# Eight of the sixteen states of a selective scan moved into the linear attention before it

## The chip, the cores and the metric

The kernel runs on one core of a Trainium2 chip. The metric is the device time of one execution in microseconds (us). The engines are named as the profile names them: PE (TensorE matmuls; PEld its weight loads), DVE (VectorE), ACT (ScalarE), POOL (GpSimd) and SP (SyncE, which here only issues DMAs). Each engine works through its own instructions in order, and semaphores tie them together.

## What is computed

Eight blocks follow one another on x of shape (4, 1024, 128), each as `x = layernorm(x + block(x))`: a gated recurrence, a routed slot memory, a sampled attention, a gated feed-forward, and then the four that matter here. All of it is float32.

```python
# L2 attention: causal linear attention, 16 heads of 64, over T positions
S += k_t[:, None] * v_t[None, :];  out_t = (q_t @ S) / max(q_t @ z, 1e-6)   # cos and sin weighted
# L2 feed-forward: each row goes to 2 of 8 experts (a gated MLP), weighted sum of the two
# L3 attention: a selective scan, E = 256 channels, N = 16 states each
delta = softplus(xs @ wd1.T @ wd2.T + wd2_b);  A = -exp(A_log)
Bm = xs @ wb.T;  Cm = xs @ wc.T
def step(h, inp):
    h = exp(d_l[:, :, None] * A) * h + (d_l * x_l)[:, :, None] * b_l[:, None, :]
    y_l = einsum('ben,bn->be', h, c_l)
y = (y + xs * W_D) * silu(skip);  out = resid + y @ out_w.T
# L3 feed-forward: 8 experts with hidden size 512, kept up to a probability mass of 0.8
```

The sum over the 16 states in `y_l` has no order of its own: each state is a recurrence for itself.

## The kernel before, in words

**The linear attention** (`l2_attn`) works through 128 units: four batch elements, four quarters of 256 positions each, eight pairs of heads. A loop over t writes the PE instructions of several units in a fixed order: keys of unit t+1 (`l2_keys`), projections of t+2 (`l2_project`, tile `pqk`), scores of t+1 (`l2_scores`, tile `pa`, which DVE weights into `a` at L1122), sums of t (`l2_before`, `l2_within`, tile `po`) and of t+1 (`l2_sums`, tile `st`). In `l2_project` ACT makes `r_q` and `r_k` (L1056) and POOL multiplies `r_q` into `qt` (L1064), which `l2_before` reads two rounds later. PE's order in this part is written out by hand; every other engine's order, and all of what comes later, is made by a scheduler when the program is built, by priority and by its own idea of times.

**The pairs of the L2 feed-forward** are prepared while the attention runs. When an element's attention is finished, `l2_dispatch` routes its rows (a chain of small DVE steps) and puts each row twice into a buffer in HBM, sorted by expert: 16 indirect DMAs on POOL's queue (`xrows`, L1388), one a round. `l2_ffn` is one generator over the 92 tiles of all elements (23 each): SP loads a tile's weights (`wx`, L1463), PE, ACT and DVE compute it (`pa_m` or `ph` from `xgT`, `kp_mo` or `py` from `mh`), `yrows` goes to HBM, and `l2_combine` gathers an element's rows back: per half of an element eight indirect DMAs on POOL's queue (`yg`, L1534), scaling on ACT, an addition and a norm. Inside the attention `early` moves this generator one step a round. It waits whenever the next element has not been put, and then holds back the last eight tiles of the element before it. `m2["rest"]` is the last element's put loop.

**The scan** (`l3`) goes through eight halves (element, then 512 positions). For each, `l3_prepare` makes the norm, the convolution, the step sizes `dl`, the inputs `ud` and the rows of B and C, which go to HBM (`rows`). `l3_scan` then does 16 states, each so: SP loads one row of B and one of C to all partitions (`bn`, `cn`, L1849); POOL multiplies `db = ud * bn` (L1854, 128x1024); for each of two channel halves ACT makes the decay `da = exp(dl * aneg)` in PSUM (L1858) and DVE runs the recurrence (L1859) from `da` and `db` into `db`; POOL multiplies `hc = db * cn` (L1870). PE adds the `hc` of all states into PSUM by a matmul with the identity (`pys`); from element 1 on two states are first added by an accumulating DMA (`hc<-hc`, L1875). `l3_sum` and `l3_finish` end the half, and then its experts can start (`l3_experts`, `ph`, `hh`, `py` from `wh`, at most four steps beside one state). The first half of all is prepared inside the attention, one step a round (`l3_early`, `l3_prepare`), from the round on in which element 0's pairs are all combined (`st["done"]`); its 16 states follow after the attention. `l3_early` keeps that half's tiles in the feature copies `xT` of the elements whose attention is over.

## Time and profile before

| | us |
|---|---|
| median of 6 executions | 2316.08 (2309.01 to 2318.73) |
| the profiled execution | 2313.36 |
| its span, first to last instruction | 2311.6 |
| PE busy | 2007.9 (87%) |
| DVE busy | 1352.4 (59%) |
| ACT busy | 1192.5 (52%) |
| POOL busy | 1023.8 (44%) |

In the profiled execution the linear attention's units begin at about 614 us; their last norm ends at about 1344; the first `db` of half 0 begins at 1388.7, of half 1 at 1486.0, of half 2 at 1576.0, and the last `hc` ends at 2172.3. Times in the text are counted from the first instruction. A share of busy time is a mean over stages that have different limits, so the windows of single stages say more than the table.

### The profile page before, as it was taken

What the parts mean: (1) busy time and instruction counts of PE and PEld (TensorE: products, weight loads), DVE (VectorE), ACT (ScalarE), POOL (GpSimd) and SP (SyncE); (2) the same over time, 40 slices, a digit from 0 to 9 for tenths busy, and PEclk for the clock granted to TensorE, in tenths of its full rate; (3) what the DMA queues carried; (4) which work ended last, traced back from release to release, by engine and by line L of the source; (5) the groups of instructions that cost most, each with busy time, mean ns of one, the idle gap of its engine ahead of it and who ended that gap; (6) DMA issues with size and microseconds to landing.
All of it is one profiled execution on the core that took longest, in us unless ns stands there. A gap on an engine that the chain in (4) does not pass through costs nothing.

```text
span 2311.6 us, 46313 instructions
## 1 busy us (share of the span) xinstructions
PE 2007.9 (87%) x17788; PEld 1403.9 (61%) x17788; DVE 1352.4 (59%) x3668; ACT 1192.5 (52%) x2606; POOL 1023.8 (44%) x812
## 2 busy tenths in 40 slices
PE   6679789989999999999979866688888899898998
PEld 3555465544477777787768654346565556565666
DVE  6658544343455654654645555785776788777521
ACT  6533334322244444454555546476767886767443
POOL 5100310000123244234143337987788889888500
PEclk9668879989999999999989987799999999999999
DMA  3000110050000010021222065455676667676411
GB/s 106 0 28 10 40 38 1 19 172 0 1 3 2 3 38 22 25 88 43 76 77 79 22 202 166 123 176 168 197 219 173 173 186 199 179 196 175 118 60 51
DMA packets 138555, 211.09 MB, mean 91 GB/s; under 512 B 18596, under 2 KB 75933, under 8 KB 137950
## 3 DMA queue, kind: packets, MB, share of 16 engines
q1 hardware_dynamic: 126190, 173.87, 24.4%
q0 software_dynamic: 12144, 34.26, 7.1%
q8 instruction: 140, 2.29, 0.4%
q14 instruction: 81, 0.66, 0.1%
HBM read 160.29 MB, written 23.16 MB: 79 GB/s over the span
## 4 chain that ended last, share of the span: by engine, by line
PE 44%; DVE 13%; ACT 11%; issue 3%; another core or an unknown queue 1%; POOL 1%; DMA 1%; SPq 0%; ACTq 0%; DVEq 0%; POOLq 0%
PE py L129 8%; PE ph L129 7%; PE po L1131 5%; PE pa_m L129 5%; DVE db L1859 5%; PE pqk L129 5%; PE kp_mo L129 3%; PE pys L129 3%; PE pv L129 2%; PE pr L1201 2%; ACT hh L1985 1%; PE pt L133 1%; ACT da L1858 1%; PE kp_mo L133 1%
## 5 line engine op out<-in xcount | busy, mean ns | idle before, releaser
L1064 POOL TENSOR_TENSOR qt<-r_q,sb_c_turn 128x256 f32<-128x256 f32 (+1 forms) x256 | 164.4, 662 | 455.0 <-ACT r_q L1056 450.8
L1870 POOL TENSOR_TENSOR hc<-db,cn 128x1024 f32<-128x1024 f32 x128 | 317.6, 2516 | 84.1 <-PE pys L129 41.5
L129 PEld LDWEIGHTS py<-wh,hh 128*128 128x128 f32 x2048 | 253.5, 194 | 83.8 <-issue 45.9
L1854 POOL TENSOR_TENSOR db<-ud,bn 128x1024 f32<-128x1024 f32 x112 | 289.8, 2657 | 12.4 <-issue 9.9
L129 PE MATMUL ph<-xT,wh 128*128 128x512 f32 x512 | 255.5, 614 | 26.2 <-DVE h_acc L2001 8.4
L129 PE MATMUL py<-wh,hh 128*128 128x128 f32 x2048 | 261.2, 279 | 16.3 <-ACT hh L1985 8.0
L1985 ACT ACTIVATE hh<-ph,sb_cols 128x512 f32<-128x512 f32 x256 | 170.5, 681 | 131.9 <-PE ph L129 100.0
L1122 DVE TENSOR_TENSOR a<-pa_m,sb_c_near 128x256 f32<-128x256 f32 x256 | 96.6, 419 | 210.4 <-PE pa_m L129 198.2
L1079 ACT ACTIVATE kN<-kp_mo,sb_c_trig 128x128 f32<-128x128 f32 x448 | 129.8, 371 | 131.3 <-PE kp_mo L133 122.9
L1858 ACT ACTIVATE da<-dl,aneg 128x512 f32<-128x512 f32 x224 | 153.4, 689 | 78.3 <-DVE db L1859 74.7
L129 PE MATMUL pys<-hc,sb_c_ident 128*128 128x512 f32 x324 | 157.9, 617 | 16.8 <-POOL hc L1870 14.6
L1859 DVE TENSOR_TENSOR_SCAN db<-da,carry,db 128x512 f32<-128x512 f32 x128 | 157.1, 1265 | 13.1 <-ACT da L1858 9.4
L1859 DVE TENSOR_TENSOR_SCAN db<-da,db 128x512 f32<-128x512 f32 x128 | 149.4, 1204 | 9.3 <-POOL db L1854 5.2
L129 PEld LDWEIGHTS ph<-xT,wh 128*128 128x128 f32 x512 | 88.5, 194 | 107.7 <-issue 54.0
L2001 DVE SCALAR_TENSOR_TENSOR h_acc<-py,gt,h_acc 128x128 f32<-128x128 f32 x256 | 71.9, 342 | 131.3 <-PE py L129 129.3
L129 PE MATMUL pqk<-xT,wE 128*128 128x256 f32 x512 | 135.7, 388 | 8.3 <-ACT coT L1198 4.2
L129 PEld LDWEIGHTS pys<-hc,sb_c_ident 128*128 128x128 f32 x324 | 60.8, 200 | 79.3 <-issue 58.0
L129 PEld LDWEIGHTS pqk<-xT,wE 128*128 128x128 f32 x512 | 88.2, 192 | 21.8 <-DVE cv L1041 6.6
L1198 ACT COPY coT<-pt 128x512 f32<-128x512 f32 x64 | 37.5, 586 | 115.9 <-PE pt L133 115.9
L129 PE MATMUL po<-ht,wD 128*128 128x512 f32 x192 | 93.3, 598 | 0.0
L1131 PE MATMUL po<-cv,a 128*64 128x65 f32 x2048 | 89.2, 230 | 0.0
L844 DVE TENSOR_SCALAR ht<-ph,sb_cols 128x512 f32<-128x512 f32 x48 | 35.7, 749 | 90.3 <-PE ph L129 90.2
(453 smaller groups left out, 4311.3 us busy)
## 6 DMA issues: line engine op xcount, KB each, us to landing
wx<-in_wF SPq DMA_DIRECT2D x92, 384.0 KB
bn<-rows SPq DMA_DIRECT2D x128, 256.0 KB
cn<-rows SPq DMA_DIRECT2D x128, 256.0 KB
wh<-in_wH SPq DMA_DIRECT2D x64, 512.0 KB
hc<-hc POOLq DMA_DIRECT2D x47, 512.0 KB
xrows<-zero SPq DMA_DIRECT2D x4, 1472.0 KB
xg<-xrows SPq DMA_DIRECT2D x20, 256.0 KB
yrows<-ys SPq DMA_DIRECT2D x20, 256.0 KB
```

Of the source, the lines that this page charges most:

```text
L129: return self.nc.tensor.matmul(out=out, lhsT=lhsT, rhs=rhs, start=start, stop=stop)
L133: self.nc.tensor.transpose(out, in_, self.ident[0:n, 0:n])
L1064: nc.gpsimd.tensor_mul(u["qt"][:, m, a:], u["q"][:, a:], c2["turn"][:, m, o + a : o + 2 * P])
L1079: self.nc.scalar.activation(u["kN"][:, c, m, :], pk[:, c, :], AF.Copy, scale=trig[:, k, m : m + 1])
L1122: nc.vector.tensor_mul(u["a"][:, i, :, :], pa[i], self.c2["near"][:, None, :].to_broadcast([P, 2, P]),)
L1131: self.nc.tensor.matmul(out=u["po"][self.HALF[j], i, c, :], lhsT=lhsT, rhs=rhs, start=key not in u["begun"], stop=True, skip_group_check=True,
L1854: nc.gpsimd.tensor_mul(db, ud, bc[0])
L1858: nc.scalar.activation(da, dl[:, ec, :], AF.Exp, scale=aneg[:, j : j + 1])
L1859: nc.vector.tensor_tensor_scan(db[:, ec, :], da, db[:, ec, :], carry[:, ec, n : n + 1] if h else 0.0, ALU.mult, ALU.add,)
L1870: nc.gpsimd.tensor_mul(hc, db, bc[1])
L1985: nc.scalar.activation(ht, ph, AF.Relu, bias=self.col("h_b1", i=e * NK + k))
L2001: nc.vector.scalar_tensor_tensor(acc[:, c, :], py[:, c, :], gt[:, c, e : e + 1], acc[:, c, :], ALU.mult, ALU.add,)
```

## The change

A constant `NEARLY = 8` says how many states of half 0 are taken early. The new generator `l3_first` runs them inside the attention, after `l3_prepare`, about one step a round. Per state it has the two row loads, `db = ud * bn` on POOL, two exponentials on ACT into an SBUF tile `da`, two recurrences on DVE with both inputs in SBUF, the copy of the carry on ACT, and the multiplication by `cn` on POOL. The sum over the states is kept in SBUF (`acc`, in element 0's `xT`): state 0 is multiplied straight into it, and states 1 to 7 are added by accumulating DMAs on POOL's queue, each of which waits for the one before. `bn`, `cn`, `db` and `da` have two buffers each, in a new pool `scan` that lives as long as the attention. `l3_scan` begins at state 8 for that half, and `l3_sum` adds `acc` with two DVE additions.

To have half 0 ready earlier, element 0's pairs run to their end alone (`l2_tiles_of(0, 1)`) before those of elements 1 to 3 begin, its 16 rows are put two a round, and preparing starts when the first half of the element is combined (`st["half"]`). In `l3` half 0 has eight states; beside each of them two steps of half 1's preparation and of the last put loop are taken. `next(moe)` is called twice a state in halves 0 and 1, and once later; before, twice in half 0 and once later. The weights `wA` move out of the constants into the first stage's pool, and the pools `wd` and `w0` are opened earlier. The cut diff:

```diff
+NEARLY = 8
 # l2_attn
-            side, begin = [], None
+            side, begin, left = [], None, 4 * NEARLY
...
-                    if "done" in self.m2["st"][0]:
+                    if "half" in self.m2["st"][0]:
                         if begin is None:
-                            begin = self.l3_prepare(self.l3_early(first))
-                        next(begin, None)
+                            scan = ctx.enter_context(tc.tile_pool(name="scan", bufs=2))
+                            u = self.l3_early(first, scan)
+                            begin = chain(self.l3_prepare(u), self.l3_first(u, scan))
+                        for k in range(1 if "dl" not in u else max(1, -(-left // max(1, n - t)))):
+                            next(begin, None)
+                            left -= 1
 # l2_dispatch
-                yield
+                if k or b:
+                    yield
 # l2_ffn
+        yield from self.l2_tiles_of(0, 1, wp)
+        yield from self.l2_tiles_of(1, B, wp)
+    def l2_tiles_of(self, b0, b1, wp):
-            for st in self.m2["st"]
+            for st in self.m2["st"][b0:b1]
 # l2_combine, after each half
+            st["half"] = h
 # l3
-            for n in range(NST):
+            for n in range(u.get("start", 0), NST):
                 with self.tc.high_priority(offset=1000):
                     next(scan)
                     next(end, None)
-                    next(nxt, None)
-                for k in range(1):
+                    for k in range(1 if i else 2):
+                        next(nxt, None)
+                for k in range(1 if i else 2):
                     next(self.m2["rest"], None)
-                next(moe, None)
-                if i == 0:
-                    for k in range(1):
-                        next(moe, None)
+                for k in range(2 if i < 2 else 1):
+                    next(moe, None)
 # new
+    def l3_first(self, u, pool):
+        nc, aneg = self.nc, self.c3["aneg"]
+        dl, ud, rows, acc, carry = (u[k] for k in ("dl", "ud", "rows", "acc", "carry"))
+        for n in range(NEARLY):
+            bc = []
+            for i, nm in enumerate(("bn", "cn")):
+                t = pool.tile([P, 1, 512], F32, name=nm)
+                r = i * NST + n
+                nc.sync.dma_start(
+                    out=t[:, 0, :], in_=rows[r : r + 1, :].to_broadcast([P, 512])
+                )
+                bc.append(t.to_broadcast([P, 2, 512]))
+            yield
+            db = pool.tile([P, 2, 512], F32, name="db")
+            nc.gpsimd.tensor_mul(db, ud, bc[0])
+            yield
+            for ec in range(2):
+                j = ec * NST + n
+                da = pool.tile([P, 512], F32, name="da")
+                nc.scalar.activation(da, dl[:, ec, :], AF.Exp, scale=aneg[:, j : j + 1])
+                nc.vector.tensor_tensor_scan(
+                    db[:, ec, :], da, db[:, ec, :], 0.0, ALU.mult, ALU.add
+                )
+            nc.scalar.copy(carry[:, :, n : n + 1], db[:, :, 511:512])
+            yield
+            nc.gpsimd.tensor_mul(db if n else acc, db, bc[1])
+            if n:
+                nc.gpsimd.dma_start(out=acc, in_=db, accum_op=ALU.add)
+            yield
 # l3_scan
-        for n in range(NST):
+        for n in range(u.get("start", 0), NST):
 # l3_sum
+            if "acc" in u:
+                self.nc.vector.tensor_add(p, u["acc"][:, ec, :], p)
```

More of the change, by code (lines that the diff above doesn't have):

```diff
@@ L61, with __init__ @@
 class Net:
-    def __init__(self, ctx, tc, io):
+    def __init__(self, ctx, tc, io, wd, w0):
         self.tc, self.nc, self.io = tc, tc.nc, io
@@ L70, in __init__ @@
         c = self.const
+        self.wdp = wd.enter_context(tc.tile_pool(name="wd", bufs=1))
+        self.w0p = w0.enter_context(tc.tile_pool(name="w0", bufs=1))
         self.xN = [c.tile([P, NC, D], F32, name=f"xN{b}") for b in range(B)]
@@ L81, in __init__ @@
             if b == 0:
-                self.wgru = self.load("wA", [P, 4, P])
+                self.wgru = self.load("wA", [P, 4, P], self.w0p)
                 self.cols = self.load("cols", [P, NCOLS])
@@ L1697, in l3_at, with l3_early @@
         return pool.tile(shape, F32, name=name, tag=tag)
-    def l3_early(self, pool):
-        half = lambda b, i: self.xT[b][:, i * 512 : (i + 1) * 512]
+    def l3_early(self, pool, scan):
+        half = lambda i: self.xT[0][:, i * 512 : (i + 1) * 512]
+        two = lambda x: x.rearrange("p (e t) -> p e t", e=2)
         k = [0]
         def at(name, shape):
-            if name in ("xnT", "tail", "xs3"):
+            if name in ("xnT", "tail", "xs3", "ud"):
                 return pool.tile(shape, F32, name=name)
-            if name in ("dl", "ud"):
-                return self.xT[1 if name == "dl" else 2].rearrange("p (e t) -> p e t", e=2)
+            if name == "dl":
+                return two(self.xT[1])
@@ L1710, in at @@
             if name == "sq3":
-                return half(2, 0).rearrange("p (k d) -> p k d", d=D)
+                return half(0).rearrange("p (k d) -> p k d", d=D)
             if name == "db1":
-                return half(2, 1)[0:ND]
+                return scan.tile([P, 512], F32, name="da")[0:ND]
             if name == "xc":
                 k[0] += 1
-                return half(0, k[0] % 2)
-            return half(0, name == "sp_w")[:, None, :]
-        u = dict(b=0, h=0, at=at, ff=self.bank("pj"))
+                return half(k[0] % 2)
@@ L1720, in l3_early @@
+            return half(name == "sp_w")[:, None, :]
+        u = dict(b=0, h=0, at=at, ff=self.bank("pj"), start=NEARLY, acc=two(self.xT[0]))
+        u["carry"] = pool.tile([P, 2, NST], F32, name="carry0")
         self.c3["first"] = u
         return u
+    def l3_first(self, u, pool):
[27 more added lines that the diff above has]
+            yield
@@ L1830, in l3_scan @@
         xnT, xs, dl, ud, rows = (u[k] for k in ("xnT", "xs", "dl", "ud", "rows"))
-        carry = wp.tile([P, 2, NST], F32, name="carry") if h == 0 else u["prev"]["carry"]
-        u["carry"] = carry
+        if "carry" not in u:
+            u["carry"] = (
+                u["prev"]["carry"] if h else wp.tile([P, 2, NST], F32, name="carry")
+            )
+        carry = u["carry"]
         u["py"] = py = []
@@ L2167, in program @@
     with ExitStack() as ctx:
-        n = Net(ctx, tc, io)
         wd, w0 = ExitStack(), ExitStack()
-        wdp = wd.enter_context(tc.tile_pool(name="wd", bufs=1))
-        W = n.l0_load(w0.enter_context(tc.tile_pool(name="w0", bufs=1)))
-        d = n.l1_ffn_load(wdp)
+        n = Net(ctx, tc, io, wd, w0)
+        W = n.l0_load(n.w0p)
+        d = n.l1_ffn_load(n.wdp)
         dp = ctx.enter_context(
```

## The prediction

> **What bounds the kernel now.** I read the page's 40 slices first, then the windows by stage. Columns: PE, PEld, DVE, ACT and POOL busy with instruction counts, granted clock, DMA share, GB/s.
>
> ```profile
> 614.00:1159.00 545.00, 515.30 (x9378) 419.87 (x9377) 308.86 (x1081) 250.00 (x737) 175.22 (x280) 1.00 0.11 33
> 1159.00:1210.00 51.00, 36.10 (x440) 29.62 (x439) 23.81 (x103) 29.47 (x87) 21.00 (x26) 0.83 0.25 73
> 1340.00:1486.00 146.00, 89.28 (x348) 59.51 (x347) 82.90 (x181) 77.43 (x175) 105.27 (x64) 0.74 0.54 166
> 1486.00:1806.00 320.00, 273.40 (x1305) 180.94 (x1303) 233.76 (x442) 219.00 (x423) 266.07 (x144) 0.93 0.62 180
> 1806.00:2172.00 366.00, 338.10 (x1670) 218.82 (x1671) 280.75 (x535) 263.16 (x455) 325.60 (x162) 1.00 0.69 186
> 2172.00:2312.00 140.00, 126.11 (x692) 89.31 (x690) 33.11 (x119) 56.57 (x91) 0.35 (x1) 0.96 0.18 55
> ```
>
> Until 1340 the linear attention runs, and PE sets its pace (515 of 545 us) while POOL is a third busy. From 1486 POOL and PE are both near 90% over the scans of halves 1 to 7. Between lies a hole, 1340 to 1486: PE 89 of 146 us at clock 0.74. There half 0 is scanned, and no expert of the last layer can start before it is finished. Next I read POOL's timeline in the hole (start, length, line, what ended the idle time before).
>
> ```profile
> 1369.97 0.99 POOL L1388 DMA_INDIRECT xrows<-xN,di  x1 [0.30 <-DVE wt L1382]
> 1388.69 2.35 POOL L1854 TENSOR_TENSOR db<-xT,bn 128x1024 f32<-128x1024 f32 x1
> 1399.45 0.99 POOL L1534 DMA_INDIRECT yg<-yrows,di  x1 [0.16 <-issue]
> 1409.20 6.98 POOL L1870 TENSOR_TENSOR hc<-db,cn 128x1024 f32<-128x1024 f32 x3
> 1437.11 6.96 POOL L1870 TENSOR_TENSOR hc<-db,cn 128x1024 f32<-128x1024 f32 x3 [7.59 <-DVE db L1859]
> 1486.00 9.27 POOL L1854 TENSOR_TENSOR db<-ud,bn 128x1024 f32<-128x1024 f32 x4
> ```
>
> The last element's routing ends at 1370, 30 us after the attention; 16 puts (`xrows`) hold POOL until 1390; 16 states, eight gathers and some waits take it to 1486, where half 1 begins. So the hole is POOL's, and the change halves its states. The price must be looked for before 1340.
>
> **What eight states leave out of the hole.** In the changed program's order of instructions POOL has, after the attention: 16 puts, `db` x4, `hc` x3, 8 gathers, `hc`, `db` x4, `hc` x3, 8 gathers, `hc`, then half 1. Counted from the attention's end: routing 30 as now; puts 1370.0 to 1390, 20 us, so 50; the first scan began 12.6 us after the first `db` (1388.7 to 1401.3 in DVE's rows), so 63; three states' scans took 12 us there (1401.3 to 1413.4), plus one `hc` of 2.4, so 77. Eight gathers took 10.1 (1359.9 to 1370.0): 87. One `hc` and four `db`, 11.7: 99. Three `hc`, 7.0, with 2 us for DVE (the waits there were 7.6, 1.8 and 0): 108. Gathers 10.1, `hc` 2.4: half 1 starts after 121 us, not 146, a gain of **25**. With no wait for scans it is 110 (gain 36), with the 7.6 us wait twice 131 (gain 15). The eight gathers more than now between `db` and half 1 belong to element 1, whose pairs now end later; the gain is no 8/16 of the hole for that reason. SP's loads do not push this back: `bn` and `cn` of the first four states stand behind pair tile 45's weights where they now stand behind tile 53's, and they are issued at the routing's end (1369.9) in any case.
>
> **What eight states cost in the attention.** First the attention's units, eight without pair tiles, eight with one each, then the five while element 0's pairs were combined and five like them without that.
>
> ```profile
> 811.40:850.20 38.80, 37.19 (x745) 29.92 (x745) 21.20 (x74) 16.96 (x52) 15.49 (x22) 1.00 0.16 50
> 971.50:1021.40 49.90, 49.34 (x849) 41.99 (x849) 29.34 (x105) 24.54 (x79) 15.46 (x22) 1.00 0.30 91
> 1155.00:1210.30 55.30, 40.40 (x521) 33.40 (x520) 27.86 (x126) 32.12 (x93) 22.42 (x28) 0.85 0.27 80
> 1014.50:1049.50 35.00, 32.64 (x540) 27.18 (x538) 20.10 (x69) 18.84 (x54) 13.59 (x19) 1.00 0.31 89
> ```
>
> A unit is 4.85 us, a tile adds 1.39. The new order runs 34 tiles before the last projection instead of 38: **-5.6**; the four come back in the hole, where PE has 57 us idle. The combination costs 20.3 us now, since 16 gathers stand before `qt` on POOL and ACT waits for them. It moves to units without tiles, where ACT has less else to do; I take **-4** (0 to -10). Preparing half 0 (the norm, convolution and step sizes) moves 20 units forward with the same instructions, tile-free as now: 0. Two puts a unit for element 0: 16 x 1 us spread over eight units of an idle POOL, 0.
>
> The eight states stand in units 106 to 117 of POOL's order. POOL gets 16 multiplies of 2.35 (37.6), 7 accumulating DMAs of 1.08 (row below, 7.6), beside 24 `qt` of 0.73 (17.5) and 8 puts of 0.99 (7.9): 70.6 us in units that now take 12 x 4.85 plus two tiles and a norm, about 62. DVE gets 16 scans. Today's scans read their decay from PSUM (L1859: 1.19 to 1.28 us whatever POOL does); the new ones read decay and input both from SBUF. The nearest rows with that are the first layer's:
>
> ```profile
> 13.99 1.23 DVE L237 TENSOR_TENSOR_SCAN gru_h<-gru_a,gru_z 128x512 f32<-128x512 f32 x1 [3.19 <-POOL gru_z L235]
> 40.53 1.21 DVE L237 TENSOR_TENSOR_SCAN gru_h<-gru_a,gru_z 128x512 f32<-128x512 f32 x1
> 40.78 2.03 POOL L235 TENSOR_TENSOR gru_z<-gru_z,gru_g 128x512 f32<-128x512 f32 x1 [1.90 <-ACT gru_z L231]
> 42.77 1.26 POOL L235 TENSOR_TENSOR gru_z<-gru_z,gru_g 128x512 f32<-128x512 f32 x1
> 42.84 2.27 DVE L237 TENSOR_TENSOR_SCAN gru_h<-gru_a,gru_z 128x512 f32<-128x512 f32 x1 [0.47 <-POOL gru_z L235]
> ```
>
> Alone each takes 1.2 to 1.3 us; together the later one takes 2.0 to 2.3. So the two engines' work adds: 70.6 + 16 x 1.22 = 90 us, less the 15.5 us of DMA issues that read no tile: 75 to 90, I take 80, so **+18** over 62. Behind a held scan on DVE stand `a` and `st`, which PE needs within a unit; behind a multiply on POOL stands `qt`, needed about a unit later, a slack of some 5 us that 18 us exceed. The new waits on POOL: a state's sum waits in POOL's queue until the sum before it has landed, and with two `db` buffers the multiply two states later does too, with `qt` and the puts of element 2 queued behind. Today's `hc` sums have their last packet 4.4 to 6 us after the issue, and states follow at 7 to 10 us, so I count 0 (up to 2 us x 7). On ACT 16 exponentials of 0.69 and 8 copies of 0.18, 12.5 us in units that keep it busy for 17 of 39: 0, or part of the 18 where they delay `r_q`. On SP the 16 `bn` and `cn` loads stand ahead of tile 28's weights, used some six units after the last of them can go: 0. Bounds of the whole: 0 if the slack and the gaps hide all, and 66 if nothing is hidden (8 x (2 x 2.35 + 1.08 + 2 x 1.22) = 8 x 8.2). I stay near the low end, since POOL is idle for two thirds of the attention.
>
> The Trainium skill ("SBUF — State Buffer", "Who interferes with whom") speaks against this edit: a DVE instruction with two SBUF inputs and a GpSimd instruction that reads SBUF exclude each other for a whole instruction. The rows alone would also allow that both run at half speed; a scan beside a 2.35 us multiply would then take 2.4 us, by the page up to 3.6. As an estimate by that page, up to 16 x 1.2 = 19 us more would stand on DVE, and the sum would end near no gain.
>
> **After the hole.** POOL's work from half 1 on is the same 112 states. The tiles are not spread alike: 15 and 14 in halves 1 and 2 become 30 and 0, and element 3's gathers move from half 3 to half 2. Halves 1 to 3 took 100, 108 and 112 us. PE's 81 us in half 1 become 81 + 15 x 1.74 (1.13 + 0.61 a tile in the timeline) = 107, so about 120 us; half 2 loses 24 us of PE and gains 10 of POOL, 106; half 3 loses 20 of POOL, 92 like half 4. 318 against 320: **0** (-10 to +18). POOL's wait there is PE already:
>
> ```profile
> L1870 POOL TENSOR_TENSOR hc<-db,cn 128x1024 f32<-128x1024 f32 x113 | 282.8, 2538 | 72.5 <-PE pys L129 41.5 <-DVE db L1859 11.9 <-DMA bn<-rows 8.0
> L1875 POOL DMA_DIRECT2D hc<-hc x47 | 50.7, 1080 | 0.3 <-POOL hc L1870 0.3
> ```
>
> Sixteen fewer additions on PE lie in the hole, 0; two DVE additions of 0.7 for the sum, 0 beside half 1's scans (1.4 if not). **Sum: -5.6 - 4 + 18 - 25 + 0 = -16.6.** The profiled execution took 2313.36 us (span 2311.6 and 1.8 around it), 2.7 under the median of 2316.08; the shift applied to the median gives **2299**. About 0.2% (4.6 us) is what a measurement can tell.
>
> **Rivals.** *Free cover*: the attention hides the states (+3) and scans keep ahead (-30): -37, 2279. For it: POOL's idle time; against it: the L237 rows. 0.20. *Lockstep*, the slower side: in units 106 to 117 POOL, DVE and PE wait on each other in turn, because `qt` and `a` stand in order behind each state's multiply, scan and landing of the sum before it, and the whole 8.2 us of a state is exposed: 66 - 9.6 - 25 = +31, 2347. It decides from 34.6 us exposed, 4.3 us a state. For it: the combination's 20 us came from just such queueing; against it: idle shares. 0.21. *Half 1 bound by PE*: 30 tiles hold it and half 2 gives nothing back: +18, 2317, no change. 0.11. My forecast has 0.48, its own range 2284 to 2313.
>
> Faster: 0.46 + 0.20 + 0.01 = 0.67; same: 0.02 + 0.08 + 0.01 = 0.11; slower: 0.20 + 0.02 = 0.22. The range reaches into lockstep and free cover: 2274 to 2328.
>
> **What would show it.** Right: attention longer by some 8 us in all, units 106 to 117 near 80 us; scans in SBUF at 1.2 to 3.6 us; hole near 121 us; no pair tile after half 1. Wrong: units 106 to 117 over 97 us, or half 1 over 135 us with half 2 still over 105.

## The result, and the profile after

The changed kernel takes 2324.14 us (22 executions) against 2316.99 (46) before: a ratio of 1.0031 (95% interval 1.0021 to 1.0042), slower, where 2299 was forecast. Its profiled execution took 2323.88 us against 2313.36. The stages below are cut at the same rows of both traces: first projection of the attention (`pqk`), end of its last output projection (`pr`), first `db` of half 1 and of half 4, end of the last multiplication `hc`, last computing instruction.

| stage, us | before | after | difference | forecast |
|---|---|---|---|---|
| up to the first projection | 614.5 | 619.2 | +4.7 | 0 |
| attention | 724.3 | 753.1 | +28.8 | +8.4 |
| from its end to half 1 (the hole) | 147.2 | 108.1 | -39.1 | -25 |
| halves 1 to 3 | 320.6 | 319.8 | -0.8 | 0 |
| halves 4 to 7 | 365.7 | 382.1 | +16.4 | no term |
| after the last `hc` | 135.8 | 136.4 | +0.6 | no term |

The first line is within chance: runs e1 to e4 below, which share the changed kernel's code up to there and ran on one chip, began the attention between 614.7 and 621.1 us. The windows of the changed kernel (columns as before), with the first element's combination, the units with the early states, the hole, and halves 1 to 4:

```profile
1081.00:1128.00 47.00, 32.56 (x414) 23.17 (x407) 14.75 (x53) 18.36 (x55) 27.78 (x33) 0.71 0.13 39
...
1225.00:1317.00 92.00, 69.43 (x1170) 56.36 (x1169) 59.80 (x135) 41.88 (x114) 70.32 (x57) 0.87 0.38 88
...
1398.00:1480.00 82.00, 54.52 (x250) 39.06 (x250) 48.02 (x89) 46.25 (x108) 67.71 (x48) 0.78 0.68 216
1480.00:1582.00 102.00, 80.76 (x388) 57.94 (x389) 84.39 (x162) 71.36 (x155) 90.38 (x50) 0.87 0.67 200
1582.00:1705.00 123.00, 107.69 (x543) 72.11 (x542) 84.92 (x169) 83.84 (x175) 97.46 (x57) 0.96 0.68 191
1705.00:1800.00 95.00, 80.62 (x402) 52.03 (x401) 72.98 (x145) 72.78 (x122) 81.15 (x40) 1.00 0.63 171
1800.00:1910.00 110.00, 96.02 (x440) 60.14 (x440) 73.80 (x137) 74.60 (x135) 81.70 (x41) 0.95 0.62 165
```

Units 106 to 117 (1225 to 1317) take 92 us with POOL busy for 70.3. That this is near the prediction's sum of 70.6 is luck: three of the 16 multiplications ran before 1225, while the 24 `qt` took 22.3 us for the 17.5 counted, and ten puts took 12.6 where eight were counted at 7.9. Half 4 is the surprise. It has no pair tile and no gather, POOL is busy in it for 81.7 us (half 3: 81.2), and yet it takes 110. Before, POOL's same work took 92:

```profile
1690.00:1807.00 117.00, 102.93 (x506) 68.02 (x507) 81.50 (x163) 84.13 (x152) 99.86 (x59) 0.96 0.65 181
1807.00:1899.00 92.00, 86.00 (x427) 55.41 (x425) 73.64 (x144) 74.09 (x140) 81.32 (x42) 1.00 0.68 187
```

POOL's timeline in the hole (start, length, line, what ended the idle time before) follows the order that the prediction walked through:

```profile
1398.03 1.00 POOL L1394 DMA_INDIRECT xrows<-xN,di  x1 [40.13 <-DVE chd L1376]
...
1418.16 9.28 POOL L1901 TENSOR_TENSOR db<-ud,bn 128x1024 f32<-128x1024 f32 x4
1427.41 2.35 POOL L1917 TENSOR_TENSOR hc<-db,cn 128x1024 f32<-128x1024 f32 x1
...
1447.17 9.28 POOL L1901 TENSOR_TENSOR db<-ud,bn 128x1024 f32<-128x1024 f32 x4
...
1468.32 0.99 POOL L1544 DMA_INDIRECT yg<-yrows,di  x1
...
1480.42 9.27 POOL L1901 TENSOR_TENSOR db<-ud,bn 128x1024 f32<-128x1024 f32 x4
```

Half 1 starts 5.6 us earlier than before, at 1480.4. Up to there the change has a gain, though a third of the one forecast. By the start of half 4 it is 6.4 us, and half 4 loses it.

### The profile page after: what moved, and what is told of

It is laid out like the page before. It is cut to its first block, busy times and chain, and to the rows that moved or that the text cites. A ratio compares the mean times of both kernels' runs of the same rounds, so it can differ in the third digit from the quotient of the medians.

```text
span 2322.1 us, 46204 instructions
## 1 busy us (share of the span) xinstructions
PE 2003.6 (86%) x17756; PEld 1404.1 (60%) x17756; DVE 1364.1 (59%) x3662; ACT 1190.6 (51%) x2600; POOL 1037.6 (45%) x819
## 5 line engine op out<-in xcount | busy, mean ns | idle before, releaser
L1070 POOL TENSOR_TENSOR qt<-r_q,sb_c_turn 128x256 f32<-128x256 f32 (+1 forms) x256 | 169.5, 689 | 415.7 <-ACT r_q L1062 411.9
L1917 POOL TENSOR_TENSOR hc<-db,cn 128x1024 f32<-128x1024 f32 x120 | 300.2, 2508 | 77.6 <-PE pys L132 26.7
L1901 POOL TENSOR_TENSOR db<-ud,bn 128x1024 f32<-128x1024 f32 x120 | 308.8, 2610 | 22.1 <-ACT th L1954 13.0
L132 PE MATMUL py<-wh,hh 128*128 128x128 f32 x2048 | 259.1, 278 | 16.4 <-ACT hh L2034 14.9
L132 PE MATMUL pys<-hc,sb_c_ident 128*128 128x512 f32 x292 | 142.2, 613 | 6.1 <-DMA hc<-hc 4.0
L132 PE MATMUL pqk<-xT,wE 128*128 128x256 f32 x512 | 141.6, 401 | 5.6 <-ACT coT L1204 3.1
L1906 DVE TENSOR_TENSOR_SCAN db<-da,db 128x512 f32<-128x512 f32 x112 | 131.1, 1206 | 7.6 <-ACT da L1905 5.4
L132 PE MATMUL ph<-xgT,wx 128*128 128x128 f32 x408 | 65.8, 313 | 33.9 <-issue 14.5
L132 PEld LDWEIGHTS ph<-xgT,wx 128*128 128x128 f32 x408 | 60.3, 223 | 51.7 <-issue 26.5
## 6 DMA issues: line engine op xcount, KB each, us to landing
wx<-in_wF SPq DMA_DIRECT2D x92, 384.0 KB
```

The costliest lines, as they stand in the source:

```text
L132: return self.nc.tensor.matmul(out=out, lhsT=lhsT, rhs=rhs, start=start, stop=stop)
L1070: nc.gpsimd.tensor_mul(u["qt"][:, m, a:], u["q"][:, a:], c2["turn"][:, m, o + a : o + 2 * P])
L1901: nc.gpsimd.tensor_mul(db, ud, bc[0])
L1906: nc.vector.tensor_tensor_scan(db[:, ec, :], da, db[:, ec, :], carry[:, ec, n : n + 1] if h else 0.0, ALU.mult, ALU.add,)
L1917: nc.gpsimd.tensor_mul(hc, db, bc[1])
```

## The experiments

Each ratio is to the kernel before on the same chip. The sixteen runs were made on four chips; on those of runs e9 to e16 the kernel before itself takes 2276 us, so times of different groups are compared by stage or by ratio. Each stage is read from one profiled execution. The stages, in us:

| run | ratio (95% interval) | attention | hole | halves 1-3 | halves 4-7 | after |
|---|---|---|---|---|---|---|
| e1 no early states | 1.0177 (1.0159-1.0195) | 721.6 | 154.0 | 331.8 | 386.2 | 136.5 |
| e2 no sum DMAs | 1.0212 (1.0192-1.0232) | 756.8 | 100.4 | 366.0 | 386.5 | 134.6 |
| e3 decay in PSUM | 1.0002 (0.9983-1.0020) | 735.2 | 111.1 | 324.6 | 384.0 | 135.1 |
| e4 old tiles | 1.0005 (0.9988-1.0021) | 755.8 | 111.3 | 301.5 | 384.8 | 139.1 |
| e5 before, two tiles | 1.0048 (1.0030-1.0066) | 725.0 | 146.9 | 326.3 | 371.4 | 140.5 |
| e6 PSUM, order a | 0.9959 (0.9944-0.9975) | 740.2 | 108.9 | 324.3 | 382.0 | 136.3 |
| e7 PSUM, gathers, order b | 1.0124 (1.0103-1.0145) | 728.5 | 96.2 | 378.5 | 382.5 | 135.6 |
| e8 PSUM, gathers, order c | 0.9961 (0.9943-0.9979) | 729.4 | 136.9 | 312.4 | 371.4 | 135.8 |
| e9 PSUM, old tiles | 0.9956 (0.9934-0.9978) | 729.3 | 103.2 | 296.2 | 388.1 | 139.1 |
| e10 before again | 2278.07 us, one run | 718.3 | 135.1 | 307.0 | 369.7 | 135.8 |
| e11 after again | 2297.52 us, one run | 745.6 | 103.2 | 321.0 | 381.8 | 134.8 |
| e12 before, puts two | 1.0065 (1.0042-1.0088) | 717.4 | 148.2 | 298.3 | 373.9 | 141.2 |
| e13 pace after half 3 | 1.0128 (1.0079-1.0177) | 745.4 | 103.2 | 316.9 | 386.7 | 136.0 |
| e14 pace in half 4 | 1.0087 (1.0059-1.0114) | 743.0 | 103.0 | 318.0 | 386.6 | 135.1 |
| e15 e9, pace from half 2 | 0.9943 (0.9918-0.9967) | 731.4 | 103.7 | 308.4 | 376.6 | 134.8 |
| e16 e9, pace from half 3 | 0.9918 (0.9888-0.9947) | 728.7 | 103.8 | 302.7 | 371.6 | 138.6 |

**What the states cost in the attention: e1, e2, e3.**

e1: the states left in half 0, all the rest of the change kept.
```diff
-NEARLY = 8
+NEARLY = 0
-        ... start=NEARLY, acc=two(self.xT[0]))
+        ... start=0)
-                            begin = chain(self.l3_prepare(u), self.l3_first(u, scan))
+                            begin = self.l3_prepare(u)
```


> Nothing is taken early: no state is scanned in the attention, half 0 has its sixteen again; the first element still drains alone and half 0 is still prepared early. In the changed kernel the last projection ends at 1372.3 us (before: 1338.8) and half 1 starts 108.1 us later (before: 147.2). Theory A (the eight states are what lengthens the attention: POOL's and DVE's work add up in units 106 to 115, 30 us over the length without them): the last projection ends near 1372 - 30 = 1342, half 1 starts some 145 us after it, so near 1487 as before. Rival B (it is the draining alone and the early preparation, not the states): the last projection stays after 1360. On the later loss (half 4, 109 us where before takes 92): if it comes from the states it is gone here; if it comes from the tiles (30 and 0 in halves 1 and 2) it stays; if it is only how the scheduler happened to put half 5's preparation among the experts, it may be in any half or in none. Total by A without the half 4 loss 2317, with it 2333.

The attention is 31.5 us shorter than in the changed kernel and 2.7 shorter than before: theory A. In units 106 to 115 the time over plain units of the same place is 2.3 us, in the changed kernel 30.3. But the total is not that of theory A: it is 31 us above the changed kernel. Only some 14 us of this lie where the states are (the attention 31.5 shorter, the hole 45.9 longer); the other 16 lie in halves 1 to 7, whose scans are the same, so the states can be credited with 14 and not with 31. Without states the hole is 6.8 us longer than before, halves 1 to 3 are 11.2 longer and halves 4 to 7 are 20.5 longer. So the later loss is there without any early state, and the rest of the change is enough for it.

e2: the accumulating DMAs left out.
```diff
-            if n:
-                nc.gpsimd.dma_start(out=acc, in_=db, accum_op=ALU.add)
```


> Leaves out the seven accumulating DMAs of the early states (states 1 to 7 are missing from the first half's sum). Theory A (POOL's compute and DVE's scans shut each other out): the DMAs are 7 x 0.96 us of POOL's queue and read no tile, so units 106 to 115 shorten by 0 to 7 us, the scans in SBUF keep a mean near 1.8 us and qt near 0.95. Rival C (the landing of a sum is what POOL, and behind it qt, waits for): units 106 to 115 lose 15 us or more. Total by A 2318 to 2324, by C 2309 or less, with half 4 as it is.

Units 106 to 115 stay 31.4 us over plain length (30.3 with the DMAs), so rival C falls: the sums' landing holds nothing up. That the total still rose by 40 us was in neither theory. The attention is 3.7 longer; the hole is shorter by 7.7; halves 1 to 3 take 46 us more. They do not hold quite the same work: eight gathers (10 us of POOL's queue) and three pair tiles that the changed kernel runs in the hole run in them here. The rest of the 46 is the same question as half 4, in a larger size.

e3: the early decay in PSUM.
```diff
-                da = pool.tile([P, 512], F32, name="da")
+                da = self.psb("pj", [P, 512], "da")
```


> The early states' decay goes to PSUM (the bank pair of the projections), so that their scans read one input from SBUF like those of the later halves. Theory A (two SBUF inputs on DVE against POOL): scans fall from a mean of 1.80 us to 1.2 to 1.3, qt from 0.95 towards 0.73, units 106 to 115 lose some 16 x 0.6 + 30 x 0.2 = 16 us, unless the bank pair makes the projections wait. Rival D (queue order, not the reads): the scans get shorter but the attention ends when it does now, or later by the waits for the bank. Total by A 2308, by D 2324 or more.

The attention loses 17.9 us, the size that theory A named; units 106 to 115 fall from 30.3 over plain length to 10.5. But the edit does two things. The scans read one input from PSUM, and, since the decay now needs the projections' banks, the states come later and further apart: the 16 scans start between 1229 and 1363 us (changed kernel 1220 to 1295), six of them in units 106 to 115, and the last two after the attention's end at 1354.3. So the 17.9 us are not all due to the reads. Attention and hole together, which hold all the early states in both kernels, are 15.0 us shorter; the halves give back 6.7, and the ratio goes from 1.0031 to 1.0002. Groups by line and form over 1190 to 1340 us (instructions | busy us, mean ns | idle before), first the changed kernel, then e3 (its other four scans come after 1340), then e1 (1190 to 1310):

```profile
L1757 DVE TENSOR_TENSOR_SCAN db<-da,db 128x512 f32<-128x512 f32 x16 | 28.4, 1803 | 4.7 <-POOL db L1751 4.6
```
```profile
L1070 POOL TENSOR_TENSOR qt<-r_q,sb_c_turn 128x256 f32<-128x256 f32 x40 | 33.5, 895 | 41.6 <-ACT r_q L1062 41.6
```
```profile
L1757 DVE TENSOR_TENSOR_SCAN db<-da,db 128x512 f32<-128x512 f32 x12 | 14.6, 1220 | 7.9 <-ACT da L1756 4.1 <-issue 3.5
```
```profile
L1070 POOL TENSOR_TENSOR qt<-r_q,sb_c_turn 128x256 f32<-128x256 f32 x47 | 34.7, 791 | 38.3 <-ACT r_q L1062 38.2
```
```profile
L1070 POOL TENSOR_TENSOR qt<-r_q,sb_c_turn 128x256 f32<-128x256 f32 x42 | 29.7, 726 | 77.4 <-ACT r_q L1062 77.4
```

A scan with both inputs in SBUF takes 1803 ns on average, with the decay in PSUM 1220; `qt` 895 against 791 and 726. How they meet is seen row by row, DVE's timeline of the changed kernel and then POOL's:

```profile
1219.51 4.53 DVE L1757 TENSOR_TENSOR_SCAN db<-da,db 128x512 f32<-128x512 f32 x2
...
1224.87 3.09 DVE L1757 TENSOR_TENSOR_SCAN db<-da,db 128x512 f32<-128x512 f32 x1
...
1228.46 1.21 DVE L1757 TENSOR_TENSOR_SCAN db<-da,db 128x512 f32<-128x512 f32 x1
...
1246.34 2.83 DVE L1757 TENSOR_TENSOR_SCAN db<-da,db 128x512 f32<-128x512 f32 x1
...
1249.15 1.21 DVE L1757 TENSOR_TENSOR_SCAN db<-da,db 128x512 f32<-128x512 f32 x1
```
```profile
1216.65 4.71 POOL L1751 TENSOR_TENSOR db<-ud,bn 128x1024 f32<-128x1024 f32 x2 [8.54 <-DVE ud L1862]
1221.30 3.26 POOL L1070 TENSOR_TENSOR qt<-r_q,sb_c_turn 128x256 f32<-128x256 f32 x2
1224.52 2.36 POOL L1762 TENSOR_TENSOR xT<-db,cn 128x1024 f32<-128x1024 f32 x1
...
1245.78 0.86 POOL L1764 DMA_DIRECT2D xT<-db  x1
1246.42 1.67 POOL L1070 TENSOR_TENSOR qt<-r_q,sb_c_turn 128x256 f32<-128x256 f32 x2
1248.26 1.80 POOL L1394 DMA_INDIRECT xrows<-xN,di  x1 [0.18 <-issue]
```

The scan at 1224.87 runs beside a multiply that lasts until 1226.88, and ends 1.08 us after it: it did next to nothing while the multiply ran, and the multiply took its usual 2.36. The `qt` pair at 1221.30 meets scans that were there first, and takes 3.26 us instead of 1.4. So it is exclusion and not half speed, and in these rows whoever comes second waits. The order of starts does not always decide: the scan at 1246.34, which began while POOL issued a DMA, ends 1.08 us after the two `qt` that began behind it. The rule of the Trainium skill that the prediction weighed ("SBUF — State Buffer", "Who interferes with whom") says just this, exclusion for a whole instruction, and all these rows agree with that.

**What halves 1 to 7 cost: e4 to e8.**

e4: one pair tile a state in half 1, as before the change.
```diff
-                for k in range(2 if i < 2 else 1):
+                for k in range(2 if i < 1 else 1):
                     next(moe, None)
```


> Half 1 takes one tile a state again instead of two, so that halves 1 and 2 have some 15 tiles each; nothing else is changed. Attention and hole as in the changed kernel. If half 4's 109 us come from moving the tiles (theory T), halves 4 to 7 go back from 382 to 366 us and the total is near 2308. If they come from the eight states' shift of the scans against the experts (theory S), they stay near 382 and the total near 2324. If it is only the scheduler's order (theory O), any half may be the long one.

Halves 1 to 3 lose 18 us, halves 4 to 7 stay at 384.8. That is not theory T as it was written, but it does not refute T: half 4 now holds the last eight gathers (10 us of POOL's queue), which the changed kernel runs in halves 1 and 2. Halves 1 to 7 together hold the same gathers and the same scans in both, and their sum answers the question. With this one edit it goes from 701.9 back to 686.3 us, what it is in the kernel before. The windows of halves 1 to 7, before, after, e4 and e5:

```profile
1486.00:2172.30 686.30, 611.80 (x2976) 399.81 (x2975) 514.58 (x977) 482.46 (x878) 591.97 (x304) 0.97 0.66 183
```
```profile
1480.40:2182.30 701.90, 617.59 (x3013) 406.50 (x3014) 521.88 (x999) 491.61 (x897) 592.58 (x304) 0.96 0.65 182
```
```profile
1488.20:2174.50 686.30, 613.78 (x2999) 400.58 (x3000) 519.22 (x984) 484.36 (x891) 592.63 (x304) 0.96 0.68 185
```
```profile
1486.20:2184.00 697.80, 611.97 (x2942) 396.38 (x2941) 512.48 (x960) 483.52 (x873) 592.06 (x304) 0.95 0.66 179
```

POOL is busy for 592 us in all four. The total fell by less, from a ratio of 1.0031 to 1.0005: of the 15.6 us, 10.5 are given back before and after these halves in the profiled execution.

e5: the kernel before, disturbed only in the pacing of its tiles.
```diff
-                if i == 0:
+                if i <= 1:
                     for k in range(1):
                         next(moe, None)
```


> The kernel of before, with half 1 at two pair tiles a state instead of one: no early state, nothing of the change. The same instructions run, and from half 4 on only their order differs from before. Theory O (halves 4 to 7 took 365.7 us in before because of the order that the scheduler had found there; any other order takes 380 or more): halves 4 to 7 take 375 to 390, the total 2322 to 2340. Rival S (what the early states or the draining alone do to the scans costs halves 4 to 7 their 16 us): halves 4 to 7 stay at 366 +- 4.

Slower by 0.48% (11 us) with nothing but another order; against before's first profile +5.7 us in halves 1 to 3, +5.7 in halves 4 to 7, +4.7 after them. Halves 4 to 7 at 371.4 lie between the two expectations. This edit is no disturbance at random: it is the change's own pacing of half 1, which e4 takes out. Taken out of the new kernel it gives 15.6 us in halves 1 to 7, put into the old one it costs 11.4 there.

e6: e3, three tiles a state in half 0 and one in half 1, one put a state.
```diff
-                for k in range(1 if i else 2):
+                for k in range(1):
                     next(self.m2["rest"], None)
-                for k in range(2 if i < 2 else 1):
+                for k in range(3 if i < 1 else 1):
                     next(moe, None)
```


> The changed kernel with the early decay in PSUM (as in the run before it) and three pair tiles a state in half 0, one in half 1. PE's order in halves 4 and 5 is then nearly that of before (2 and 4 edits in the sequence of scan, preparation and expert groups, where the changed kernel has some 10 to 20). Attention as in the run with the decay in PSUM (735 us from the first projection to the last). Theory O: halves 4 and 5 take 182 +- 6 (changed kernel 202), halves 4 to 7 some 368, total 2294 to 2300, faster than both. Rival S: halves 4 to 7 stay near 384 and the total near 2312.

A miss for theory O in its strict form: halves 4 and 5 took 100.2 and 97.5 us, not 182 together, though PE's sequence of groups was nearly that of before. The total is below before by 0.41%; in the profiled execution attention and hole together are 22 us shorter than before's and halves 1 to 7 20 us longer. So one pair tile a state in half 1 is not enough for before's halves: here 12 tiles run as late as half 3 (before 5, e4 6).

e7: e3 with the first element's gathers held to the attention's beat; three tiles a state in half 1, two after it.
```diff
-                nc.gpsimd.indirect_dma_start(
+                g = nc.gpsimd.indirect_dma_start(
...
+                if b == 0:
+                    self.tc.add_manual_dep(g, self.beat.name, SYNC, reason="spread out")
-                for k in range(2 if i < 2 else 1):
+                for k in range(2 if i < 1 else 3 if i < 2 else 2):
                     next(moe, None)
```


> Decay in PSUM; the first element's sixteen gathers are held to one beat of the attention each, so that they no longer stand eight in a row before qt on POOL; the tile pacing is one for which PE's order in halves 5, 6 and 7 is that of before, edit for edit (half 4: 14 edits). Theory G (the combination costs its 25 us because eight gathers in a row hold qt): the units of the combination lose 15 to 22 us, the attention takes 713 to 720. Rival: the gathers cost what they cost wherever they stand, 735. Theory O: halves 5 to 7 take 273.6 +- 5 as in before.

Halves 5 to 7 took 283.1, not 273.6: PE's sequence of groups alone does not fix the time; the other engines' orders differed. The attention is 6.7 us shorter than e3's, not 15 to 22. The total is 1.24% over before: half 1, with three tiles a state, takes 153.6 us.

e8: e3 with the same gathers, four tiles a state in half 0, one after it.
```diff
-                    for k in range(1 if i else 2):
+                    for k in range(1):
                         next(nxt, None)
-                for k in range(2 if i < 2 else 1):
+                for k in range(4 if i < 1 else 1):
                     next(moe, None)
```


> As the run before (decay in PSUM, gathers held to a beat each), but with four tiles a state in half 0 and one after it: PE's order is nearly that of before in halves 1 to 4 (4, 0, 0 and 4 edits) and another in halves 5 and 6 (14 and 13). Theory G: attention 713 to 720. Theory O: halves 2 to 4 take 323 +- 10 as in before, half 4 alone 92 +- 4, halves 5 to 7 more than before's 273.6. Total by both some 2285 to 2295.

Half 4 takes 95.2 and halves 5 to 7 276.2, as theory O asked; halves 2 to 4 take 307, less than its 323 +- 10, and the total is 2307.75, not 2285 to 2295: the attention stays at 729.4 and the hole grows to 136.9, where 24 pair tiles now run. POOL's timeline shows why theory G got only part of its gain:

```profile
1076.23 1.01 POOL L1544 DMA_INDIRECT yg<-yrows,di  x1 [0.69 <-issue]
...
1085.06 0.95 POOL L1544 DMA_INDIRECT yg<-yrows,di  x1 [0.30 <-issue]
...
1123.29 0.99 POOL L1544 DMA_INDIRECT yg<-yrows,di  x1 [0.15 <-issue]
1124.58 0.96 POOL L1544 DMA_INDIRECT yg<-yrows,di  x1 [0.31 <-issue]
1128.06 0.87 POOL L1070 TENSOR_TENSOR qt<-r_q,sb_c_turn 128x128 f32<-128x128 f32 x2 [2.52 <-ACT r_q L1062]
```

The second eight gathers now come two between each pair of `qt`, and the 10 us of their unit are gone, of which 5.7 come back in a later unit; the first eight still stand in a row from 1076 to 1086, and that unit still costs 11.

**Two edits together, and what repeats: e9 to e12.**

e9: the edits of e3 and e4.


> The two edits that each stood alone above, together: the early decay in PSUM, and one pair tile a state in half 1. PE's order is that of the run with the old tiles, row for row from half 0 on, so only the attention should differ from it. If stages add: attention 735 us (as with the decay in PSUM), hole 111, halves 1 to 3 301.5 and halves 4 to 7 385 (as with the old tiles), tail 136 to 139; the time is that of the run with the old tiles less 18 to 20, some 0.8% under before. Rival: what the attention saves is given back in the halves, as it was when only the decay went to PSUM (2313.6 there, no better than before): 2312 or more.

The stages come out 5 to 8 us under those expected, halves 4 to 7 3 us over: attention 729.3, hole 103.2, halves 1 to 3 296.2, halves 4 to 7 388.1 (eight gathers in half 4 again). Against the changed kernel on the same chip (e11) the attention is 16.3 us shorter and halves 1 to 3 are 24.8 shorter. It is faster than before by 0.44%, not by 0.8: on this chip before has a hole 12 us and halves 1 to 3 13.6 us shorter than in its first profile.

e10 and e11: both kernels once more.


> The kernel of before, unchanged, for a second profile. Theory K (before's halves 4 to 7 are the only ones of ten profiles in which PE's clock is never lowered, and that is a property of the kernel, not of the one execution): halves 4 to 7 take 366 +- 3 with a clock of 1.00 in all four. Rival N (chance of the execution): clock under 1.00 in one of them and 370 or more.

> The changed kernel, unchanged, for a second profile. Theory K: half 4 is the long one again, 107 to 112 us with a clock near 0.95, halves 4 to 7 take 382 +- 4. Rival N: any half, or none.

Half 4 after: 109.0 us (first 109.3), halves 5 to 7 92.6, 94.5 and 85.7, halves 5 to 7 to a tenth as in the first profile. Before: 94.6, 89.9, 97.3 and 87.9 (first 92.1, 89.9, 97.3 and 86.4). Single lengths here belong to the kernels, within 2.5 us. Of theory K for the kernel before this is all that holds: the clock in e10 was below 1.00 in three of the four halves, and the sum of 369.7 us lies between the two expectations. Halves 1 to 3 repeat less well: before's half 2 takes 105.9 us here and 113.7 in the first profile, half 3 110.8 and 117.0. So on this chip the change costs 26 us in halves 1 to 7 (676.7 and 702.8), 14 of them in halves 1 to 3, and its one execution is 0.9% over before's median, where the first comparison had 0.31%. POOL's timeline around the end of half 4, after, e11 and before:

```profile
1893.02 2.34 POOL L1917 TENSOR_TENSOR hc<-db,cn 128x1024 f32<-128x1024 f32 x1 [8.16 <-PE pys L132]
...
1909.49 6.97 POOL L1901 TENSOR_TENSOR db<-ud,bn 128x1024 f32<-128x1024 f32 x3 [12.96 <-ACT th L1954]
```
```profile
1868.40 2.34 POOL L1917 TENSOR_TENSOR hc<-db,cn 128x1024 f32<-128x1024 f32 x1 [8.24 <-PE pys L132]
...
1884.68 6.97 POOL L1901 TENSOR_TENSOR db<-ud,bn 128x1024 f32<-128x1024 f32 x3 [12.76 <-ACT th L1954]
```
```profile
1882.15 2.98 POOL L1870 TENSOR_TENSOR hc<-db,cn 128x1024 f32<-128x1024 f32 x1
1889.24 4.68 POOL L1870 TENSOR_TENSOR hc<-db,cn 128x1024 f32<-128x1024 f32 x2 [4.11 <-PE pys L129]
1895.89 2.36 POOL L1870 TENSOR_TENSOR hc<-db,cn 128x1024 f32<-128x1024 f32 x1 [1.97 <-DVE db L1859]
...
1898.79 4.97 POOL L1854 TENSOR_TENSOR db<-ud,bn 128x1024 f32<-128x1024 f32 x2
```

The changed kernel waits twice, 8.2 us for a sum on PE and some 13 before half 5, in both executions; before waits 4.1 and 2.0 us, and before half 5 not at all. PE's timelines, after and then before, show the queue that this comes from:

```profile
1882.70 1.13 PE L132 MATMUL ph<-xT,wh 128*128 128x512 f32 x2 [1.50 <-DVE h_acc L2050]
1885.54 3.73 PE L132 MATMUL pdb<-xs,sb_s_e 128*97 128x512 f32 x4 [1.71 <-ACT hh L2034]
1889.06 1.91 PE L132 MATMUL ph<-xT,wh 128*128 128x512 f32 x2
1890.77 2.16 PE L132 MATMUL pys<-hc,sb_c_ident 128*128 128x512 f32 x4
...
1894.29 1.02 PE L132 MATMUL pd<-db,sb_s_d 65*128 65x512 f32 x2
```
```profile
1877.01 1.96 PE L129 MATMUL pdb<-xs,sb_s_e 128*97 128x512 f32 x4 [0.24 <-ACT hh L1985]
...
1881.53 2.09 PE L129 MATMUL pd<-db,sb_s_d 65*128 65x512 f32 x4 [0.18 <-DVE gt L1944]
...
1887.23 1.88 PE L129 MATMUL pys<-hc,sb_c_ident 128*128 128x512 f32 x4
```

In both kernels a sum (`pys`) that frees POOL's buffer stands behind half 5's `pdb`. The difference is in `pd`, from which half 5's `ud` is made. After the change it comes 8.75 us after `pdb`, at 1894.29, when POOL's last `hc` of half 4 is under way (1893.02); POOL then has nothing left to do until `ud` is there. Before it comes 4.52 us after `pdb`, at 1881.53, and POOL still has four `hc` of half 4 before it (1882.15 to 1898.25).

e12: the kernel before, with two puts a state in half 0.
```diff
-                for k in range(1):
+                for k in range(2):
                     next(self.m2["rest"], None)
```


> The kernel of before with the last element's puts two a state in half 0 instead of one: the same instructions, another order in halves 1 to 7 (some 15 to 23 edits in each). Theory O in the form that is left (any other order opens waits of PE that lower its clock in halves 4 to 7): 371 to 387 us there with 2 to 13 us lost to the clock, and the total over before's. Rival: a reordering costs nothing where the work is the same, 366.

Slower by 0.65% (15 us). Against e10, the hole is 13.1 us longer, halves 1 to 3 are 8.7 shorter, halves 4 to 7 4.2 longer, and what follows is 5.4 longer. The first two belong together: 32 pair tiles and 24 gathers run in the hole, where before has 19 and 16. Like e5 this is an edit of the change's own, two puts a state in half 0, in the old kernel. The lowered clock does not set the length of halves 4 to 7: one less the granted clock, times the length, is 18.7 us here (over the 2 to 13 expected) at 373.9 us, and 8.5 in the changed kernel at 382.1.

**Pacing alone: e13 to e16.**

e13, e14: the changed kernel, with one edit each.
```diff
-                for k in range(4 if n % 8 == 7 else 3):
+                for k in range(4 if n % 8 == (5 if i > 2 else 7) else 3):            # e13
+                for k in range(3 + 2 * (n == 15) if i == 4 else 4 if n % 8 == 7 else 3):   # e14
                     next(work)
```


> The changed kernel with one edit: from half 3 on, the extra step of the expert groups in each eight states comes at the sixth state instead of the eighth. Up to half 3 everything is as in the changed kernel: attention 745 to 753, halves 1 to 3 320 +- 3. Theory O (order in PE's queue alone): half 4 and the sum of halves 4 to 7 move by 5 us or more from 109 and 382, and half 4's waits of POOL with them. Rival S (something the early states leave behind): 109 +- 2 and 382 +- 3 again.

> The changed kernel with one edit: in half 4 alone both extra steps of the expert groups come at the last state. PE's order is that of the changed kernel in halves 0 to 3, 8 edits away in half 4 and some 25 in halves 5 to 7. Theory O: halves 5 to 7 leave their 92.6, 94.5 and 85.7 us, each by 2 us or more, and half 4 its 109. Rival S: 109 +- 2 again.

e13: half 4 107.4 and half 6 100.6 (e11: 109.0 and 94.5), 4 to 7 386.7; just short of the 5 us that theory O asked of the sum. e14: halves 4 to 7 104.8, 100.6, 89.8 and 91.4 against 109.0, 92.6, 94.5 and 85.7: three halves move by 4.7 to 8.0 us, half 4 by 4.2. Rival S falls: with nothing changed upstream, every one of the four moves. Neither order is a better one in sum: halves 1 to 7 take 703.6 and 704.6 us, with e11 702.8.

e15, e16: the same kind of edit on e9.
```diff
-                for k in range(4 if n % 8 == 7 else 3):
+                for k in range(4 if n % 8 == (6 if i > 1 else 7) else 3):   # e15
+                for k in range(4 if n % 8 == (0 if i > 2 else 7) else 3):   # e16
                     next(work)
```


> The version with the early decay in PSUM and one pair tile a state in half 1 (ratio 0.9956 above; its halves 4 to 7 took 388), with the extra step of the expert groups at the seventh state from half 2 on. Attention, hole and half 1 as there. Theory O: halves 4 to 7 anywhere from 366 to 390; at 370 the ratio to before is 0.988. Rival: 388 +- 3.

> The same version with the extra step at the first state of each eight from half 3 on: halves 1 and 2 as there, PE's order in half 5 within 3 edits of that of before (there 90 us), in half 4 14 edits away. Theory O: half 5 near 90 and halves 4 to 7 under 388. Rival: 388 +- 3.

e16's windows (halves 1 to 3, halves 4 to 7):

```profile
1443.00:1746.00 303.00, 268.17 (x1358) 181.05 (x1359) 240.20 (x462) 220.11 (x434) 268.12 (x146) 0.96 0.71 200
1746.00:2118.00 372.00, 343.21 (x1653) 222.88 (x1652) 279.05 (x525) 262.82 (x453) 324.08 (x160) 0.97 0.67 178
```

Halves 4 to 7 fall from 388.1 to 371.6 (e15: 376.6), half 5 to 90.1, the length it has before. Part of this is a move: the eight gathers of half 4 run in half 3 in both runs, and halves 1 to 3 grow by 6.5 (e15: 12.2). Halves 1 to 7 take 674.3 us (e15: 685.0) against 684.3 in e9, so this pacing gains 10 us in one run and none in the other. With 0.9918 e16 has the lowest ratio here, below both kernels; e15's interval overlaps with its own.

## Why the prediction was wrong, point by point

- **After the hole, forecast 0 (-10 to +18), and nothing for halves 4 to 7.** This step failed. The prediction argued from amounts ("POOL's work from half 1 on is the same 112 states"), let pair tiles move from half 2 to half 1 at no price, and took for granted that an unchanged instruction list keeps its time. POOL's busy time did stay (592.0 and 592.6 us in halves 1 to 7); the seven halves went from 686.3 to 701.9. Halves 1 to 3 kept their sum (319.8 against 320.6), and halves 4 to 7 took 16.4 us more. What the runs showed in its place: the pacing of the tiles, an edit beside the states, has a price. With one tile a state in half 1 the halves are back at 686.3 (e4), with two a state in the old kernel they take 697.7 (e5); by the ratios it is some 0.3 to 0.5%. Order alone can do nearly as much: pacing the experts differently moved single halves by up to 8 us (e14) and the sum by 10 (e16).
- **The base of that step was misread as well.** Half 1 before ends at 1576.0, not at 1586, so halves 1 to 3 took 90, 114 and 117 us and not 100, 108 and 112, and PE was busy in half 1 for 71 us, not 81; the tiles in them are 13, 12 and 5 (after: 22, 11 and none). Half 1, forecast at 120, took 101, half 2 123 for 106.
- **States in the attention, forecast +18, measured 28.** Direction and place were right, the term was too small: units 106 to 117 took 92 us (80 forecast, 97 the mark for wrong). One part of it is the exclusion of DVE and POOL. As an estimate from the mean durations, it holds the 16 scans for 9 us (1803 against 1220 ns) and the 40 `qt` for 7 (895 against 726 ns in e1). Without it and with the states further apart, attention and hole lose 15.0 us (e3); what each of the two would give alone was not tested. The half speed that the prediction left open is ruled out by its own rows: beside each other, the scan at 40.53 and the multiplication at 42.77 keep the 1.21 and 1.26 us that they take alone, and only the later instruction grows. The prediction's estimate by the Trainium skill's page, up to 19 us more on DVE, is a bound that was not reached, with 9. Adding all of POOL's work and all scans gave 90 us, close to the 92; the step down to 80 took off the DMA issues as if no scan could hold them, and two puts beside scans took 1.80 and 1.74 us instead of 0.99. The new waits behind the sum's landing, counted at 0, are 0 (e2). The rest of the 28 us, beyond the exclusion's 16, is open.
- **Combination, forecast -4, measured +3 to +5.** It costs 24.9 us over plain units after the change; before, 20.3 by the prediction's count, and 21.8 against the same place one element earlier (five projections, `pqk`, 33.5 us). Free units did not help: the gathers still stand in a row before `qt`. **Tiles -5.6**: right, four fewer. **Preparation 0**: what remains of the attention's +28.8 is some +2 to +3.
- **The hole, forecast -25, measured -39.1** (in the second pair of profiles, e10 and e11, -31.9). The walk through POOL's order was right, with both groups of eight gathers behind the puts. The routing took 25.7 us and not 30 "as now", the first scan came 6.5 us after the first `db` (1424.6) and not 12.6, and the rest up to half 1 took 55.8 and not 58. Why the first two were shorter was not tested.
- **Rivals.** Lockstep's price was not reached: 28 us of states exposed, where it decides from 34.6. Free cover did not occur. Of half 1 bound by PE the size came near (+18 there, +15.6 in halves 1 to 7) and the place did not: the loss lies in half 4, far behind the change.

Forecast were -16.6 us; the profiled executions differ by +10.5. The attention missed its forecast by +20.4, the halves by +15.6, the hole by -14.1, and what lies before and after by +5.3. Without either of the first two misses the sum would have been a gain of 5 to 10 us; the hole's error, in the other direction, was luck. With both edits, the decay in PSUM and one tile a state, the kernel is faster than before by 0.44% (e9).

What stays open: how much of the attention's loss is the reads and how much the density of the states (e3 changes both), and which entry of the queues decides a half's length. PE's sequence of groups alone does not (e6, e7), and e6 shows that one tile a state in half 1 does not by itself bring before's halves back. Nor was the price of draining element 0 alone measured by itself.

## What to carry to other kernels

Where a scheduler orders the queues, an edit has two prices: that of its instructions, and that of a new order for everything behind it. Put the companion edits of a change into the old kernel one at a time: here two of them, which add no instruction, cost 0.48 and 0.65% (e5, e12), near the 0.7% that the whole change was to gain. Compare the sum of the stages that share work, since tiles and gathers move from one to the next, and a single stage only with what an unchanged kernel shows: between its two profiles before's hole differs by 12 us and its halves 1 to 3 by 13.6. Take such an idea apart before dropping it: with the early decay in PSUM and the tiles paced as before the kernel beat both others. Work moved beside GpSimd should leave one of a DVE instruction's inputs out of SBUF.

## What the runs showed of the hardware that was not expected

- A lowered PE clock needs no long gap. In the changed kernel the granted clock was 0.57 from 1884 to 1892 us. The idle times of PE just ahead, up to 1882.70 and up to 1885.54, were 1.50 and 1.71 us, with 1.13 us of matmuls between. `pdb` then took 3.73 us, before the change 1.96.
- POOL's indirect puts are held by DVE's scans as well: the put at 1248.26, beside scans, took 1.80 us, in the hole one takes 0.96 to 1.00. The Trainium skill ("SBUF — State Buffer", "Who interferes with whom") says that a DMA which seems stalled by a DVE instruction is one whose descriptors GpSimd makes, and the row agrees; it also says that a probe saw this with copies and not with `tensor_tensor`, and here a scan with two inputs from SBUF is enough.
- Halves 5 to 7 of the changed kernel repeat to a tenth of a us in its two profiles (92.6, 94.5 and 85.7), though the kernel as a whole differs by 26 us between them. Its halves 1 to 3 differ by 1.3 to 2.5 us (101.4, 122.9 and 95.6; 98.9, 124.2 and 97.9).
